# A four-layer graph network on one core: first weights loaded beside their zero blocks, layer 3's small weights ahead of the graph's second copy, pair 14's layer 3 by rows, both ends reordered

## The chip, the cores and the metric

The kernel runs on one core of a Trainium2 chip. The metric is the device time of one execution in microseconds (us), as the median of several runs.

## The reference, cut to what matters

The input `x` holds 32 batches of 512 nodes with 64 features; `adj` is one graph of 512 x 512 weights, mostly zeros. Four layers follow one another; each normalises its input, clips it at zero, and adds its result to it.

```
for f in (L0, L1, L2, L3):
    h = max(layernorm(x), 0);  x = x + f(h, adj)
L0: v = h, row 0 set to intervention_value
    3 times: v = relu([v, adj @ v] @ W1.T + b1) @ W2.T + b2
L1: 2 times: z = relu((adj @ z) @ weights[i])
L2: 8 heads: y = z @ Wh;  s = (y @ y.T) * adj, zeros -> -1e16
             head = softmax(s) @ y + bh
    cat = leaky(heads, 0.01);  once more such a layer, with W_out and b_out;  leaky 0.01
L3: adj's diagonal set to 1;  y = z @ weight
    e = leaky(y @ a[:64] (of the row) + y @ a[64:] (of the column), 0.2) * adj
    out = softmax(e) @ y + bias
```

## The kernel before, in words

Batches are handled in 16 pairs, numbered 0 to 15. All work is cut into small jobs with a pair and a name (`12.r4g`), and the order of the jobs is written out by hand, as three strings. `HEAD` lists the start (pairs 0 to 3), `ROUND` lists one steady round with a lag for each pair, and `TAIL` lists the end (from the middle of pair 12's heads on). The jobs issue their instructions in this order; each engine and each DMA queue then works through its own instructions in that order, so a job's place decides what waits behind it. `UNTIL` says up to which job a TensorE accumulator bank is held.

**Start.** `x` of pair 0 and the graph `A` are loaded on the SP queue, the weights `W1` and `W2` of layer 0 on the ACT queue. `W1n` and `W2n` hold each weight twice on the diagonal of a 128-wide tile, so GpSimd zeroes the two tiles first (L305) and the four loads follow (L310, L311). On SP follow the biases, `x` of pair 1, `NP`, `Wh`, then `A2` (a second copy of the graph, in another arrangement, L333), the small weights of layer 3 (`w3bd` L335, `a12` L337, six DMAs), `Wo_sb` (L338) and `A3` (a third copy, L340). The front of pair 0 runs batch by batch as two chains of 35 steps, `A0` to `A34` and `B0` to `B34` (layernorm, three steps of L0 with L648, L687 and L654 on TensorE, two of L1, layernorm, turning). The other pairs' fronts are `F0` to `F32`. `weights`, `joined`, `biases`, `bjoined`, `graph0` to `graph3` (L367: the graph turned), `masks`, `factor0` to `factor3` (L394, on `A2`), `loops0` to `loops3` (on `A3`), `grams` and `vectors` are one-time jobs; `vectors` (L425 to L436) makes layer 3's vectors out of `w3bd` and `a12`. `k`, `Y` make keys; the first attention scores are `0.s1a` and `0.s0a`.

**Attention of a unit** (letters `a` to `j`: pairs of heads; `f`: L2's output layer; `e`: L3). `s` are the scores in PSUM (L777 and the mask L780), `r` the product with the graph and the row maximum on VectorE (L786), `m` the negative on GpSimd (L799), `x` the exponentials with their sums on ScalarE (L806), `n` the division on GpSimd (L818), `t` 32 x 32 block transposes on VectorE (L824), `v` the weighing on TensorE with 32-row tiles (L833, L1061), from values that SP's DMAs have spread (`ZQ`, `hQ`, `lQ`). `w`, `y`, `o`, `c` apply `Wh`, bend, project with `W_out` and join. `f` and `h` make the operands of the output layer, `vAE`... `er` its sums, together with L3 of the pair before. `oA` to `oV` are L3's layernorm, turning and values; `oD`, `oF` and `de` send the column terms through DRAM into a broadcast tile `pd`, from which `s` of L3 is made on ScalarE (L1015).

**Last pairs.** Pair 15's output layer (`O0`, `O1`) and layer 3 (`L0`, `L1`) run by batch and *by rows*: 128 rows at a time, `s` from a `pd` that TensorE makes in PSUM (L1252, L1258), `r` with 128-row tiles of the graph (`aO`, `aL`, L1283), `m` on VectorE (L1141), `x` (L1145), `t` a full turn on TensorE (L1152), `e` its copy, half by ScalarE and half by VectorE (L1156, L1157), `v` the weighing with K = 128 (L1165), and the division on the way out (`z`, `q`, L1175, L1176). Layer 3 of pair 14 has no later pair to share its sums with, and runs alone by columns as the unit `e` does: `vAL` to `vDL` (L833, 128 columns), `lu` (L1026), `lt` (L491), `lr` (L1042).

Of the kernel before, what the change touches and what calls it, by code (L numbers as in the profile page):

```python
# [21 lines left out]
def gnn_stack_kernel(  # L22
# [50 lines left out]
        0.r2b 1.F7 0.ZQ02 0.m0a 0.r3b 0.r4a 0.ZQ12 0.x1a 0.x0a 0.nAa 0.r5a 0.m1b 0.s3a 0.t0a 1.F8 0.t1a 0.Y1 0.r6a
        0.r7a 0.s2b 0.ZQ01 0.r5b 0.r4b 1.F9 0.m2a 0.x1b 0.m3a 0.s0b 0.s3b 0.x3a 0.B33 1.F10 0.r0b 0.r1b 0.m2b 0.s3c
        0.r7b 0.ZQ00 0.m0b 0.x2a 0.r6b 0.B34 0.nBa 0.s0c 0.r7c 0.r6c 0.r1c 0.s1c 0.x0b 0.m3b 0.nAb 0.t2a 1.F11 0.r3c
        0.r0c 0.r2c 0.t3a 0.m1c 0.x3b 0.x2b 0.ZQ13 0.k2 0.m0c 0.x0c 0.loops3 1.F12 1.F13 0.nBb 0.t0b 0.t1b 0.s2c
        0.t2b 0.x1c 1.F14 0.ZQ03 0.s0d 0.t3b 0.m3c 0.nAc 0.r4c 0.Y2 0.r5c 0.r1d 0.vA0 0.r0d 0.m2c 0.s3d 0.s1d 0.r7d
        0.t0c 0.x2c 0.vB0 0.r3d 0.m0d 0.vC0 0.r2d 0.m1d 0.r6d 0.m3d 0.vD0 0.x0d 2.F1 0.x1d 0.x3c 0.nAd 0.t1c 0.s2d
        0.us0 0.s0g 0.w00 0.x3d 0.w10 0.nBc 0.r5d 0.r4d 0.m2d 0.y00 0.t1d 0.s1g 0.x2d 0.t0d 0.t2c 1.F15 0.r2g 0.nBd
        0.r3g 0.y10 0.t3c 1.F16 0.t2d 0.m1g 0.o0 0.t3d 1.F17 0.c0 1.F18 0.s3g 0.vA1 0.vB1 1.F19 0.r6g 0.x1g 0.r1g  # L80
        0.r0g 0.vC1 0.m0g 2.F2 0.vD1 0.x0g 0.loops2 0.ZQ10 0.s2g 1.F20 0.r7g 0.s0h 0.us1 0.r4g 1.F21 0.w11 0.r5g
        0.m2g 0.r1h 0.s2h 0.nAg 0.r0h 0.m3g 0.s3h 0.x2g 0.y11 0.k3 3.F0 0.m0h 0.r4h 0.x3g 0.r6h 1.F22 0.t0g 0.r5h
        0.Y3 0.m2h 0.s1h 0.nBg 0.r7h 0.t1g 0.x0h 1.F23 1.F24 1.F25 0.t2g 0.r3h 0.w01 0.r2h 0.s1i 0.m1h 0.y01 0.s0i
        0.x1h 0.x2h 0.t3g 0.r3i 0.ZQ11 0.o1 0.m3h 0.r2i 0.x3h 0.nAh 1.F26 0.r1i 0.r0i 0.c1 0.t0h 0.s3i 1.F27 0.nBh
        1.F28 0.t1h 0.t2h 0.t3h 0.m1i 0.s2i 1.F29 0.vA2 0.vB2 1.F30 0.r6i 0.r7i 0.m0i 0.r4i 0.D0 0.m3i 1.F31 0.vC2
        0.x1i 0.x3i 0.vD2 0.x0i 0.s2j 1.F32 0.r5i 3.F1 0.m2i 0.us2 0.nAi 1.zT 1.zE 0.s1j 1.ZQ01 0.x2i 0.r5j 0.r4j
        0.r2j 0.r3j 0.t1i 0.w12 0.y12 0.s3j 0.m1j 0.nBi 2.F3 0.x1j 2.F4 0.s0j 1.k0 0.r6j 1.Y0 0.m2j 0.w02 0.r0j
        0.hQ1 0.r1j 0.y02 0.r7j 0.t0i 1.s1a 1.r3a 2.F5 0.m0j 0.x0j 1.ZQ02 1.s3a 0.o2 2.F6 0.t3i 1.r6a 1.r2a 0.m3j
        1.s0a 3.F2 0.c2 0.nAj 0.t2i 1.r7a 0.x2j 1.k1 0.x3j 0.nBj 1.r1a 2.F7 2.F8 1.Y1 1.r0a 1.m1a 1.s0b 1.s2a 0.t1j
        0.t0j 1.m0a 1.m3a 0.t2j 0.t3j 0.vA3 1.x0a 1.r5a 1.r4a 1.s3b 1.r0b 1.r1b 1.s1b 0.vB3 1.x1a 1.m2a 1.x2a 1.nAa  # L90
        1.r6b 0.hQ0 0.vC3 1.r2b 1.r7b 1.r3b 1.m1b 0.vD3 1.t0a 1.m0b 1.t1a 1.x3a 1.x1b 1.s2b 1.nBa 1.x0b 1.s0c 1.r4b
        1.nAb 1.r5b 1.t2a 0.us3 0.w03 0.y03 1.s2c 1.r1c 0.w13 1.m2b 0.loops1 0.y13 1.r5c 1.m3b 1.r4c 2.F9 1.r0c
        1.t0b 1.m0c 1.s3c 1.x3b 2.F10 1.x2b 1.x0c 1.s1c 2.F11 1.r3c 0.o3 1.t1b 1.nBb 2.F12 1.r2c 2.F13 1.m2c 1.r6c
        1.ZQ03 1.r7c 1.m3c 1.t3a 1.t2b 1.m1c 1.t3b 1.ZQ00 0.c3 1.s0d 1.s1d 2.F14 1.x3c 1.vA0 1.x1c 1.x2c 1.vB0 1.r1d
        1.nBc 1.r3d 0.f1 1.r0d 1.s3d 0.D1 1.r2d 1.m1d 1.vC0 1.vD0 1.x1d 0.f0 1.nAc 1.t2c 1.m0d 1.r7d 0.hQ3 1.t1c
        1.s2d 1.r6d 1.x0d 0.s1f 1.nAd 1.us0 1.r4d 1.r5d 1.t0d 1.w10 0.s2f 1.t0c 1.y10 1.w00 1.y00 1.m2d 1.m3d 0.r3f
        0.r5f 1.t1d 1.x2d 2.F15 0.r4f 1.o0 1.x3d 1.t3c 1.nBd 0.r2f 2.F16 1.c0 1.ZQ13 0.s0f 1.t2d 2.F17 1.t3d 1.k2
        0.m1f 0.s3f 2.F18 0.m2f 0.r1f 1.Y2 4.F0 0.x1f 0.r0f 0.r7f 1.vA1 0.r6f 1.vB1 0.m0f 1.vC1 2.F19 4.F1 2.F20
        0.x0f 1.vD1 1.s1g 1.us1 1.r3g 0.m3f 1.r2g 1.k3 1.s0g 1.r0g 1.m1g 0.x2f 1.s3g 1.w11 2.F21 1.r1g 0.nAf 1.r6g
        1.r7g 1.Y3 1.s2g 1.s1h 1.w01 1.m3g 1.m0g 0.hQ2 1.r5g 1.r4g 0.x3f 0.nBf 1.r3h 1.y11 1.s2h 1.r2h 1.m2g 1.x0g  # L100
        1.x1g 1.x2g 1.y01 0.t0f 1.x3g 1.r4h 1.r5h 1.s0h 2.F22 0.t3f 2.F23 1.o1 1.ZQ12 0.t1f 1.nAg 1.r0h 2.F24 0.t2f
        1.m1h 2.F25 1.r1h 1.c1 1.m2h 1.x1h 1.m0h 1.s3h 1.t0g 0.vAE 1.r6h 1.nBg 1.r7h 1.x0h 1.t1g 1.m3h 0.vBE 1.x2h
        1.s1i 1.t2g 1.s0i 1.nAh 1.x3h 1.r2i 1.r0i 1.r1i 1.r3i 0.vCE 0.vDE 1.s2i 1.m1i 0.eu 1.nBh 2.F26 1.ZQ11 1.t0h
        1.t3g 1.t2h 2.F27 0.et 1.t3h 2.F28 1.t1h 0.er 2.F29 2.F30 1.s3i 1.x1i 1.r7i 1.ZQ10 1.m0i 1.vA2 1.r5i 1.r4i
        1.vB2 1.vC2 1.r6i 1.vD2 1.m2i 2.F31 1.s2j 1.D0 1.s1j 1.x2i 1.x0i 1.us2 2.F32 1.r5j 1.m3i 2.zT 3.F3 1.r2j
        1.s3j 1.nAi 2.zE 3.F4 1.r3j 1.r4j 1.t0i 1.w12 1.x3i 1.nBi 1.w02 1.r6j 1.m1j 1.f0 1.s0j 1.y12 2.k0 1.y02
        1.t1i 1.r0j 1.r1j 1.r7j 0.loops0 1.m2j 2.Y0 3.F5 1.t2i 1.m0j 2.s3a 1.x1j 1.m3j 2.s1a 2.r6a 2.r7a 1.hQ0 2.r3a
        1.x0j 2.r2a 1.t3i 1.o2 2.m1a 3.F6 1.x2j 1.x3j 1.hQ1 1.nAj 2.s0a 1.c2 2.r1a 1.nBj 2.r0a 1.t0j 2.k1 1.t1j
        2.m3a 1.t2j 2.s2a 2.Y1 1.t3j 2.r4a 2.m0a 3.F7 2.r5a 2.ZQ02 2.m2a 3.F8 2.x3a 2.x0a 0.oA 2.s0b 1.vA3 2.r1b
        2.r0b 2.x1a 2.nAa 2.x2a 0.oB 2.m0b 2.nBa 1.vB3 2.ZQ03 1.vC3 1.vD3 1.us3 2.s1b 3.F9 2.t0a 1.w03 1.y03 2.t1a  # L110
        2.r2b 2.r3b 3.F10 2.s3b
# [27 lines left out]
        12.r4g 11.nBf 12.r6g 11.t0f 11.t1f 11.t2f 12.r5g 13.F23 12.x1g 12.c1 12.m3g 11.t3f 13.F24 14.F2 12.s0h  # L139
        12.r0h 12.m2g 13.F25 12.r1h 10.lQ2 12.m0h 12.x2g 12.s1h 12.nAg 11.vAE 12.r3h 12.r2h 12.t0g 12.x3g 12.m1h  # L140
        12.x0h 11.vBE 12.nBg 12.t1g 11.vCE 12.x1h 11.vDE 15.aO1 12.t2g 12.s3h 12.nAh 12.t3g 12.r7h 12.s2h 12.r6h
        12.r4h 12.r5h 11.eu 12.t0h 12.k3 12.t1h 11.et 12.m3h 12.Y3 12.m2h 11.er 12.s0i 12.r1i 12.x2h 12.s1i 12.x3h
        12.nBh 13.F26 12.r3i 12.r0i 12.r2i 12.s3i 13.F27 12.m0i 12.t2h 13.F28 12.t3h 13.F29 12.s3j 12.vA2 12.m1i
        13.F30 12.vB2 12.r7j 13.F31 12.vC2 12.vD2 12.r7i 12.x0i 12.x1i 12.r6j 12.s2i 13.F32 12.r6i 12.us2 13.zT
        12.r4i 12.f0 12.r5i 12.m3i 13.zE 12.s0j 12.s2j 12.m2i 14.F3 12.r1j 12.x3i 12.nAi 12.r4j 12.r5j 12.x2i 12.s1j
        14.F4 12.t0i 15.aL3 13.k0 13.Y0 13.ZQ00 12.m2j 12.r0j 12.w12 13.ZQ02 12.nBi 13.s3a 15.aO2 12.w02 12.t1i
        12.r3j 12.y12 12.m3j 13.r6a 12.m0j 14.F5 13.s2a 12.x2j 12.r2j 12.y02 13.r7a 12.m1j 12.x0j 13.m3a 13.s0a
        12.D0 12.t3i 13.r5a 13.r4a 12.o2 13.r0a 12.hQ0 13.s1a 13.r1a 12.x1j 13.s3b 12.x3j 12.c2 12.nAj 14.F6 12.t2i
        13.r2a 13.m2a 13.r3a 13.x3a 13.x2a 12.nBj 13.k1 13.r6b 13.r7b 12.t1j 13.m1a 13.m3b 12.t0j 13.m0a 13.nBa
# [154 lines left out]
    for z0 in (W1n, W2n):  # L304
        nc.gpsimd.memset(z0, 0.0)  # L305
# [3 lines left out]
    for r in R:  # L309
        nc.scalar.dma_start(out=W1n[r, :, r], in_=W1.rearrange("o (k d) -> o k d", k=2))  # L310
        nc.scalar.dma_start(out=W2n[r, r], in_=W2)  # L311
# [20 lines left out]
    for r in R:  # L332
        nc.sync.dma_start(out=A2[r], in_=adj.rearrange("(s q) m -> q s m", q=D))  # L333
# [1173 lines left out]
```

## Time and profile before

| | |
|---|---|
| runs shown | 2047.02, 2047.13, 2048.74 us; median 2047.13 |
| profiled execution, its own time | 2046.44 us |
| its span | 2044.7 us (1.7 us lie around it) |
| TensorE busy | 1998.0 us, 98% |
| VectorE, ScalarE, GpSimd busy | 1818.6, 1497.2, 1289.9 us |
| granted TensorE clock, mean | 0.992 |

Rows of windows give, for a stretch of the span: its length, then the busy time and instruction count of each engine, the granted TensorE clock, the busy share of the DMA engines, and GB/s. Rows of the timeline give start, length, engine, line, operation, tile written and read, count, and in brackets the idle time of the engine before it and what ended it. The chain of waits is followed back from the last instruction. Several matmuls are recorded twice (one of 512 columns in four-byte numbers counts as two).

### The profile page before, as it was taken

To read this page: it belongs to the slowest core of one execution; us is meant where nothing else is said; L and a number is where in the kernel's file an instruction comes from. 1 tells how busy PE (TensorE), PEld (TensorE's weight loads), DVE (VectorE), ACT (ScalarE), POOL (GpSimd) and SP (SyncE) were. 2 spreads that over 40 slices of the span, in tenths; PEclk is the share of its full clock that TensorE was granted. 3 is DMA by queue.
4 is the path that set the end of the run, shared out by engine and by line. 5 is a ranking of instruction groups with operands and counts; after the bars stand their busy time and mean duration, and the time that the engine had idled before them with its cause. 6 is when DMAs were issued, how large, how long until landed. Compare 5 with 4: busy or idle time off the path is not lost.

```text
span 2044.7 us, 90579 instructions
## 1 busy us (share of the span) xinstructions
PE 1998.0 (98%) x38701; PEld 1196.2 (59%) x38701; DVE 1818.6 (89%) x4247; ACT 1497.2 (73%) x3866; POOL 1289.9 (63%) x2193
## 2 busy tenths in 40 slices
PE   6999999999999999999999999999999999999997
PEld 4555565665656556565665655566565565655555
DVE  4888889999898999989999998999989899899967
ACT  1567668777787777878777787877778677787856
POOL 2476665766667575776658666675766567566541
PEclk9999999999999999999999999999999999999998
DMA  6101111102121110212111121111112111022101
GB/s 140 28 2 31 26 31 36 38 20 44 25 43 29 34 38 17 45 28 41 34 29 34 26 44 29 37 37 25 39 26 42 41 34 32 16 46 44 38 15 37
DMA packets 247224, 71.61 MB, mean 35 GB/s; under 512 B 230052, under 2 KB 239396, under 8 KB 246820
## 3 DMA queue, kind: packets, MB, share of 16 engines
q1 hardware_dynamic: 246368, 65.72, 15.5%
q8 instruction: 303, 4.96, 1.0%
q14 instruction: 101, 0.83, 0.1%
q10 hardware_dynamic: 452, 0.10, 0.0%
HBM read 14.49 MB, written 4.26 MB: 9 GB/s over the span
## 4 chain that ended last, share of the span: by engine, by line
PE 91%; DVE 4%; ACT 2%; POOL 1%; DMA 1%; issue 1%; SPq 0%; ACTq 0%; POOLq 0%; DVEq 0%
PE s L777 24%; PE mm L833 23%; PE s L780 6%; PE mm L894 5%; PE mm L536 5%; PE mm L874 5%; PE mm L1061 5%; PE mm L513 5%; PE mm L1294 3%; PE mm L539 2%; DVE sm L786 2%; PE mm L561 2%; DVE sm L824 2%; PE mm L501 1%; PE mm L530 1%
## 5 line engine op out<-in xcount | busy, mean ns | idle before, releaser
L806 ACT ACTIVATE sm<-sm,nmx 128x512 f32<-128x512 f32 x1264 | 898.3, 717 | 162.6 <-POOL nmx L799 161.0
L818 POOL TENSOR_SCALAR sm<-sm,rs 128x512 f32<-128x512 f32 x1264 | 852.3, 693 | 223.4 <-DVE rs L816 193.3
L786 DVE CUSTOM_DVE_ANT_0 sm<-s,A 128x512 f32<-128x512 f32 x1264 | 804.4, 679 | 43.6 <-PE s L780 39.9
L824 DVE STREAM_TRANSPOSE sm<-sm 128x1024 f32<-128x1024 f32 x632 | 765.3, 1229 | 52.5 <-POOL sm L818 49.6
L777 PE MATMUL s<-ZZ,Y 64*64 64x512 f32 x3840 | 510.8, 596 | 1.1 <-ACT Y L1305 0.9
L833 PE MATMUL mm<-sm,vq 32*64 32x256 f32 (+1 forms) x16640 | 484.0, 377 | 5.7 <-DVE sm L824 5.3
L833 PEld LDWEIGHTS mm<-sm,vq 32*64 32x64 f32 x16640 | 382.1, 132 | 120.6 <-issue 49.3
L799 POOL TENSOR_SCALAR nmx<-mx 128x2 f32<-128x2 f32 x632 | 128.6, 214 | 325.6 <-DVE mx L786 293.4
L806 ACT ACTIVATION_READ_ACCUMULATOR sm<-sm,nmx 128x1 f32 x1264 | 244.1, 193 | 0.0
L780 PE MATMUL s<-NEGM,I2b 64*64 64x512 bf16 x2288 | 237.1, 377 | 0.0
L777 PEld LDWEIGHTS s<-ZZ,Y 64*64 64x64 f32 x3840 | 131.3, 133 | 144.7 <-issue 64.8
L886 ACT ACTIVATE y<-mm,cols 128x512 f32<-128x512 f32 x256 | 161.3, 687 | 30.8 <-PE mm L874 30.8
L780 PEld LDWEIGHTS <-I2b 64*64 64x64 bf16 x2288 | 78.5, 107 | 153.3 <-issue 152.7
L456 POOL TENSOR_TENSOR r<-ve,mhalf 128x8 f32<-128x8 f32 (+1 forms) x68 | 108.3, 1593 | 89.1 <-DVE ve L454 84.8
L874 PE MATMUL mm<-us,Wh 64*64 64x512 f32 x1024 | 132.9, 590 | 0.9 <-ACT us L868 0.9
L868 ACT COPY us<-mm 128x256 f32<-128x256 f32 x256 | 76.0, 381 | 73.2 <-PE mm L833 73.0
L894 PE MATMUL mm<-y,Wo_sb 128*64 128x256 f32 x1024 | 124.1, 384 | 2.5 <-ACT Y L1305 2.5
L1061 PE MATMUL mm<-sm,vq 32*64 32x256 f32 x3712 | 111.0, 376 | 1.4 <-POOL nmx L799 0.2
L513 PE MATMUL mm<-AT,z 128*128 128x512 f32 x240 | 111.0, 605 | 0.1
L536 PE MATMUL mm<-AT,v 128*64 128x256 f32 x960 | 110.2, 382 | 0.0
L1061 PEld LDWEIGHTS mm<-sm,vq 32*64 32x64 f32 x3712 | 99.9, 132 | 16.2 <-PE s L780 7.9
L786 DVE DVE_READ_ACCUMULATOR2_ANT mx<- 128x1 f32 x1280 | 106.3, 83 | 0.0
(203 smaller groups left out, 1961.7 us busy)
## 6 DMA issues: line engine op xcount, KB each, us to landing
vq<-z SPq DMA_DIRECT2D x512, 32.0 KB
HH<-cat SPq DMA_DIRECT2D x128, 64.0 KB
vq<-catT SPq DMA_DIRECT2D x240, 32.0 KB
vq<-h3n SPq DMA_DIRECT2D x240, 32.0 KB
A<-in_adj_dram SPq DMA_DIRECT2D x5, 1024.0 KB
xt<-in_x_dram SPq DMA_DIRECT2D x32, 128.0 KB
ZZ<-ZZ SPq DMA_DIRECT2D x30, 128.0 KB
pd<-dst SPq DMA_DIRECT2D x30, 128.0 KB
```

Of the source, the lines that this page charges most:

```text
L513: nc.tensor.matmul(pe, lhsT=v[:, m].rearrange("p j d -> p (j d)"), rhs=AT[:, m, :], start=(m == 0), stop=(m == NT - 1),)
L536: nc.tensor.matmul(ph[out_, :], lhsT=v[:, m, j, :], rhs=AT[:, m, h], start=False, stop=stop)
L777: nc.tensor.matmul(pss[half][R[ab], :], lhsT=lhsT, rhs=rhs, start=True, stop=False)
L780: nc.tensor.matmul(pss[half][R[ab], :], lhsT=I2b[R[half], :], rhs=NEGM[R[half], k, :], start=False, stop=True)
L786: nc.vector.tensor_tensor_reduce(self.sm[:, s, :], self.pss.pop(s), self.graph(s), 1.0, -FMAX, ALU.mult, ALU.max, self.small("mx", slice(s ...
L806: nc.scalar.activation(self.sm[:, s, :], self.sm[:, s, :], AF.Exp, bias=self.small("nmx", slice(s, s + 1)), accum_out=self.small("ssum", s ...
L818: nc.gpsimd.tensor_scalar(self.sm[:, s, :], self.sm[:, s, :], self.small("rs", slice(s, s + 1)), 1.0, ALU.mult, ALU.mult)
L824: nc.vector.transpose(out=two, in_=two)
L833: nc.tensor.matmul(self.u[i][R[c], 0 : weights.shape[1] * 32], lhsT=values[32 * i : 32 * i + 32, jb, :], rhs=weights[32 * i : 32 * i + 32, ...
L874: nc.tensor.matmul(self.py[ab][c][r, :], lhsT=Wh2[R[c], self.head(c, ab), r], rhs=self.us[R[c], 2 * ab : 2 * ab + 2].rearrange("p i (s e) ...
L894: nc.tensor.matmul(self.pa[R[half], 0 : N // 2], lhsT=Wo_sb[:, self.head(k, ab), :], rhs=self.y[self.head(k, ab)][:, half * N // 2 : (half ...
L1061: nc.tensor.matmul(self.u[i][r, 0 : N // 2], lhsT=values[q, jb, :], rhs=unit.sm[q, :, 32 * jb : 32 * jb + 32], start=(jb == 0), stop=(jb = ...
```

## The change: what it does

1. The zero blocks of `W1n` and `W2n` are filled beside the weights, not under them; the four loads no longer follow the fill.
2. On SP the six DMAs of `w3bd` and `a12` are issued ahead of the two of `A2`.
3. Layer 3 of pair 14 runs by rows, as new units `M0` and `M1` of the class `HalfLast`. Its `oD`, `oF`, `de`, `e` jobs, `lQ` and `vAL` to `lr` are gone.
4. `HEAD` and `TAIL` are written anew; `ROUND` is the same. `vectors` moves from its place between `0.B4` and `0.B5` to the late part of `HEAD` (pair 1's heads).

```diff
-    for z0 in (W1n, W2n):
-        nc.gpsimd.memset(z0, 0.0)
+    for r, other in zip(R, R[::-1]):
+        nc.scalar.dma_start(out=W1n[r, :, r], in_=W1.rearrange("o (k d) -> o k d", k=2))
+        nc.scalar.dma_start(out=W2n[r, r], in_=W2)
+        nc.gpsimd.memset(W1n[r, :, other], 0.0)
+        nc.gpsimd.memset(W2n[r, other], 0.0)
     make_identity(nc, ident)
...
-    for r in R:
-        nc.scalar.dma_start(out=W1n[r, :, r], in_=W1.rearrange("o (k d) -> o k d", k=2))
-        nc.scalar.dma_start(out=W2n[r, r], in_=W2)
...
-    for r in R:
-        nc.sync.dma_start(out=A2[r], in_=adj.rearrange("(s q) m -> q s m", q=D))
     for j, r in enumerate(R):
         nc.sync.dma_start(out=w3bd[r, r], in_=w3)
         for k in range(2):
             nc.sync.dma_start(out=a12[r, 2 * k + j : 2 * k + j + 1], in_=a3[k * D : (k + 1) * D, :])
+    for r in R:
+        nc.sync.dma_start(out=A2[r], in_=adj.rearrange("(s q) m -> q s m", q=D))
...
+            if self.p == NPAIR - 2:
+                for j, pn in enumerate(self.pns):
+                    s["src", j] = st.tile([P, NT], F32, tag="src", bufs=4, name="src")
+                    nc.vector.tensor_copy(s["src", j], pn[:, :, D])
+                    nc.scalar.copy(h3n[:, :, j, :], pn[:, :, :D])
+                    s["h3n", j] = h3n[:, :, j, :]
+                return
...
     class HalfLast(Half):
         def targets(self):
             self.pd = score_ps()
+            own = R[self.j] if self.p < NPAIR - 1 else R[0]
             for r in R:
                 nc.tensor.matmul(
-                    self.pd[r, :], lhsT=w3d[R[0], R[0]], rhs=state[self.p]["zT3", self.j], start=True, stop=True
+                    self.pd[r, :], lhsT=w3d[own, own], rhs=state[self.p]["zT3", self.j], start=True, stop=True
                 )
...
+                first = HalfLast(p - 1, j, "M", "rowsL", "h3n")
+                job(p, f"dM{j}", first.targets)
+                job(p, f"b3M{j}", first.biased)
...
-        unit_jobs(p, "e", last)
-        job(p, "de", last.targets)
+        if p < NPAIR - 2:
+            unit_jobs(p, "e", last)
+            job(p, "de", last.targets)
...
-        if p == NPAIR - 2:
-            sum_jobs(p, "L", last)
-            for name, fn in (("lu", last.evict), ("lt", last.rows), ("lr", last.residual)):
-                job(p, name, fn)
```

The new start up to the first scores, and the stretch of the new end around pair 15's last join:

```
0.A0 0.B0 0.weights 0.A1 0.joined 0.A2 0.A3 0.A4 0.biases 0.B1 0.A5 0.A6 0.graph2 0.graph1 0.graph3 1.F0
0.graph0 0.bjoined 0.B2 0.A7 0.B3 0.A8 0.A9 0.B4 0.A10 0.B5 1.F1 0.B6 0.A11 0.masks 0.B7 0.A12 1.F2 0.A13
0.B8 0.A14 0.A15 0.factor0 0.A16 0.B9 0.A17 0.B10 0.B11 0.A18 0.A19 0.B12 0.B13 0.A20 0.B14 0.B15 0.factor3
0.A21 0.A22 0.B16 0.factor1 0.A23 0.B17 0.B18 0.A24 0.A25 0.A26 0.A27 0.B19 0.A28 0.grams 0.B20 0.loops2
0.A29 0.A30 0.A31 0.loops1 0.B21 0.A32 0.B22 0.B23 0.A33 0.A34 0.B24 2.F0 0.B25 0.k0 0.B26 0.Y0 0.factor2
0.ZQ00 0.B27 2.F1 0.ZQ03 0.s1a 0.s0a
...
14.oC 15.w03 15.w13 15.r3O0 15.y03 15.y13 15.t0O0 15.x2O0 15.m3O0 15.e0O0 14.oT 14.oE 15.o3 14.oN 15.t1O0
15.dM0 15.x3O0 15.c3 15.t2O0 14.oV 15.e1O0 15.t3O0 15.s2M0 15.e2O0 15.e3O0 15.v0O0 15.v2O0 15.r2M0
```

The first scores stood in the old `HEAD` behind `0.B30` and `1.F5`. In the old `TAIL` pair 13's layer 3 began `13.de 15.y00 13.s3e 15.t3d 13.r3e 13.s7e 13.r7e`; in the new it begins `13.de 14.m1f 15.w00 15.w10 15.y00 15.nBd 14.r6f 15.y10 15.t1d 15.k3 15.t2d 15.Y3 13.s0e 15.t3d 13.s3e 13.r0e`, and its eight `r` stand ahead of `14.s0f`.

## The prediction

> **What bounds the kernel now.** The page first: TensorE is busy for nearly the whole span, so the time is its work plus the places where it stands still or runs slowly.
>
> ```profile
> PE 1998.0 (98%) x38701; PEld 1196.2 (59%) x38701; DVE 1818.6 (89%) x4247; ACT 1497.2 (73%) x3866; POOL 1289.9 (63%) x2193
> ```
>
> TensorE idles for 2044.7 - 1998.0 = 46.7 us. The waits of TensorE between 100 and 1850 us sum to 2.7 us, so nearly all of it lies at the two ends. The windows of the start:
>
> ```profile
> 0.00:8.30 8.30, 0.00 (x0) 0.01 (x1) 4.28 (x13) 1.77 (x3) 3.81 (x16) 1.00 0.60 170
> 8.30:23.50 15.20, 12.62 (x96) 8.95 (x96) 6.60 (x17) 2.31 (x7) 3.69 (x5) 1.00 0.80 168
> 23.50:28.60 5.10, 0.06 (x3) 0.05 (x1) 0.25 (x1) 0.63 (x2) 0.00 (x0) 0.97 1.03 148
> 28.60:36.00 7.40, 6.81 (x57) 3.83 (x57) 2.59 (x10) 0.66 (x3) 3.14 (x3) 0.56 0.98 218
> ...
> 50.00:66.30 16.30, 12.70 (x258) 8.18 (x255) 11.49 (x30) 4.17 (x12) 5.28 (x4) 1.00 0.05 10
> ```
>
> TensorE stands for 5.0 us before 28.6, and works at a clock of 0.56 in the 7.4 us behind it. Its waits name the causes, and the chain of waits shows that the second one sets the end:
>
> ```profile
> PE mm L357 <- DMA early<-in_L_gnn_b_dram: 8.3, 1, 8.3
> PE mm L427 <- DMA early<-in_L_gnn_weight_dram: 5.0, 1, 5.0
> PE mm L367 <- DVE b1s L387: 2.2, 1, 2.2
> ```
> ```profile
> 17.42 10.92 DMA early<-in_L_gnn_weight_dram
> 28.34 0.25 issue
> 28.58 0.46 PE mm L427
> ```
>
> L427 is `vectors`, standing in TensorE's order ahead of pair 0's front, and its weight is queued behind the 2 MB of `A2`. From 66.3 to 100 us TensorE is busy for 33.35 of 33.7 us. The windows of the end:
>
> ```profile
> 1905.00:1911.00 6.00, 3.26 (x19) 0.71 (x14) 6.00 (x16) 4.95 (x9) 1.05 (x4) 0.84 0.22 46
> 1911.00:1916.30 5.30, 4.92 (x32) 2.29 (x40) 5.02 (x15) 5.30 (x15) 1.14 (x4) 0.54 0.26 53
> ...
> 1987.50:2002.00 14.50, 13.05 (x104) 8.82 (x97) 8.33 (x38) 7.47 (x24) 0.00 (x0) 1.00 0.28 66
> 2002.00:2011.00 9.00, 6.12 (x42) 4.71 (x43) 8.48 (x31) 8.94 (x24) 2.17 (x4) 0.83 0.34 73
> 2011.00:2020.00 9.00, 4.07 (x20) 2.27 (x16) 8.52 (x18) 5.80 (x15) 6.25 (x10) 0.50 0.00 1
> 2020.00:2026.70 6.70, 6.24 (x249) 6.00 (x250) 4.11 (x16) 2.66 (x7) 1.73 (x2) 0.62 0.02 5
> ```
>
> Pair 15's last join (`c3`) ends at 1987.5. In the 57.2 us behind it TensorE works 43.6 us (the four rows from 1987.5, 10.81 to 2038, 3.31 to the end). Between 2011 and 2026.7 the column form of pair 14's layer 3 holds it up, as the timeline shows:
>
> ```profile
> 2016.05 2.69 POOL L818 TENSOR_SCALAR sm<-sm,rs 128x512 f32<-128x512 f32 x4 [0.75 <-DVE src L1244]
> ...
> 2020.07 6.21 PE L833 MATMUL mm<-sm,vq 32*64 32x128 f32 x248 [1.97 <-DVE sm L824]
> ...
> 2026.67 0.63 PE L1222 MATMUL mm<-ident,z 128*64 128x128 f32 x4 [0.39 <-ACT yT L1026]
> ```
>
> Division on GpSimd, block turns on VectorE and 256 small matmuls follow one another; pair 15's last turn (L1222), whose operand is ready at 2023.4, stands behind them.
>
> **The first weights.** Their loads start on the ACT queue at 1.06 behind the fill; SP's first load starts at 0.72. At most 0.3 us goes; 1 MB of `A` is queued in between and the landing at 8.2 follows that, so I take 0.3, between 0 and 1.5 (`z` of the first batch is ready at 7.5, 1.7 us before its turn at 9.2). The smaller fills cost nothing: GpSimd then idles for 2.9 us before 5.26.
>
> **Layer 3's small weights ahead of `A2`.** SP spends 0.90 + 1.76 + 0.59 + 1.23 = 4.5 us on the six, so `A2` issues at 17.7, not 13.2. The DMA engines are full until about 28, so it lands between 28 and 30. Behind it on SP are `Wo_sb`, `A3` and pair 2's `x`, needed much later. `factor0` on VectorE is first to read `A2`; the old order reached it at 37.2, the new one some 8 us earlier, about when `A2` lands. If the landing is later, pair 0's front waits behind it for up to 2 us; taken at nothing, since the windows leave VectorE idle for over half of 28.6 to 36.
>
> **`vectors` moved.** The wait goes (5.0), and so does 28.34 to 30.76, 2.4 us, of which 0.46 + 0.56 + 0.63 = 1.65 us of matmuls stay, now where TensorE is full: 0.8 net. With the gap goes the slow clock: in the chain the next 64 x 64, 64 x 256 and graph matmuls took 0.64 + 0.85 + 3.34 where the same later took 0.46 + 0.43 + 1.88: 2.1 us. [...]
>
> **The start reordered.** `F0`, which kept VectorE waiting for pair 1's `x`, now stands behind three of the graph's turns: 2.2 us of L367's wait go. What is late next is batch A's own chain. The first scores now stand ahead of `B28`, `F3` and `F5`, so 0.46 + 0.65 + 0.77 us of filler and the 1.65 of `vectors` are missing from the stretch that already idles 3.6 of 16.3 us. I give back 2.4 us, nearer to the 2.6 idle in 8.3 to 23.5; the ends are 0 and 7.4, double that idle. Start: 0.3 + 5.0 + 0.8 + 2.1 + 2.2 - 2.4 = **8.0**, between 3.0 and 10.4.
>
> **The end up to `c3`.** Between 1898 and 1916.3 TensorE idles 0.88 + 2.74 + 0.38 = 4.0 us, and the 4.92 us at clock 0.54 hold 4.92 x 0.46 = 2.3 too much. VectorE waited there for `pd` of pair 13 (landing at 1905.05) with other maxima behind it. The new order puts 0.62 + 3 x 1.16 = 4.1 us of VectorE work between the issue and the first maximum, but then eight maxima (5.0 us) ahead of `14.s0f`, against 1.9 + 0.9 of projection and keys on TensorE. I take **2.5** of the 6.3, with ends +6.3 and, if a like stall arises in another pair, -4.
>
> **Pair 14 by rows.** TensorE loses L833 7.1, L491 0.6, L979 0.3. It gains eight turns at 0.55 (L1152 x8 took 1.09), eight weighings at 0.92 (32 records took 3.68) and two `dM` at 1.03 (L1252 at full clock): 4.4 + 7.4 + 2.1. That is **5.9 us more** on the bounding engine, and not hidden by itself. VectorE: L824 4.9, L816, L963, L984, L1042 out (6.5); L1157, L1141, L1175, L1176 in (3.3 + 1.2 + 1.2 + 2.3 + 0.3): +1.8. ScalarE: +3.1 copies, -1.1. GpSimd loses 5.7. On SP 23 DMAs go (four `src`, one `dst`, two `pd`, sixteen `lQ`), which stood ahead of later graph rows. The gain is in waits: the first score can follow `oV` (1989.3) instead of `pd` (2002.6), and nothing needs division or block turns before weighing. Behind `c3`: 43.6 + 5.9, less 2.2 for the clock (L1252 1.97 against 1.03, L1232 1.97 against 1.10, L1222 1.02 against 0.63), less 2.1 of turns and `dM0` now ahead of `c3`, where TensorE is full, is 45.2; VectorE has 39.3 + 1.8 = 41.1. Idle was 13.6, of which 3.4 (last row and store) stay; I add 3.6 for hand-overs between the three interleaved chains, nearest to the 1.45 and 2.88 idle of the first two rows. 45.2 + 7.0 + 2.1 = 54.3 against 57.2: **2.9** gained; with idle 4.0 it is 5.9, with 13.6 it is 3.7 lost. A new wait: `r2M0` on VectorE stands behind `oV` and ScalarE's `s2M0`, and `O0`'s divisions and `O1`'s maxima queue behind it; should it come late, the hand-over falls into the 3.6.
>
> [...]
>
> **Sum.** 8.0 + 2.5 + 2.9 = 13.4. The profiled execution took 2046.4 (span 2044.7, 1.7 around it), so 2033.0; the median of the runs is 0.7 above it, so **2033.7**.
>
> **The rivals.** *A, the row form pays for nothing:* its 5.9 us stay and the idle time with them, because maxima of three units now share VectorE, already 8.5 of 9 busy from 2002 on, and `dM0` and `dM1` hold two of the four score buffers. 8.0 + 2.5 - 3.7 = 6.8: 2040.3. *B, another wait takes the place of `vectors`:* batch A's chain of copies and layernorms binds. 3.0 + 2.5 + 2.9 = 8.4: 2038.7. For it: the 3.6 us idle at 50 to 66.3 are such waits. *C, both ends at their best:* 10.4 + 6.3 + 5.9 = 22.6: 2024.5. *D, slower:* in the new `TAIL` the run of eight maxima with four block turns, 8 x 0.67 + 4 x 1.2 = 10.2 us on VectorE, starves TensorE in two more of the pairs 11 to 13: 20.4 - 8.0 - 2.9 = 9.5 slower, 2056.6. It decides once new idle time before `c3` exceeds 10.9 + 4.1. For it: VectorE is busy for 51 of 55.7 us from 1916 to 1972. Against: TensorE's waits in the old order show one such place. *E, gains and the 5.9 cancel:* 2047.
>
> **How the numbers follow.** Forecast 0.52 (own range 2028 to 2038), A 0.13, B 0.13, C 0.10, D 0.07, E 0.05. The range 2022 to 2043 leaves out D, E and the far side of C, some 0.15. About 0.2% (4.1 us) can be told from no change: faster than 2043.0 are the forecast, B, C and most of A, 0.86; E and the rest of A 0.07; slower 0.07.
>
> **What would show it.** Right: no TensorE wait on the weight's DMA near 28 us, a clock of 0.9 or more from 28 to 36, first scores near 58 (66.3 before); idle under 3 us around pair 13's layer 3; L833 gone behind `c3`, TensorE near 50 us busy in the last 54. Wrong: first scores after 63, a wait for `A2` in VectorE, a new wait of TensorE for L786 between 1600 and 1987, or over 10 us idle behind `c3`.

## The result and the profile after

The changed kernel takes 2039.3 us (median of 5 runs, 2037.58 to 2040.0); the kernel before took 2048.35 us beside it. The ratio is 0.9955, 95% interval 0.9944 to 0.9966: 9.05 us faster, where 13.4 were forecast. The profiled execution took 2039.3 us, span 2037.5.

Busy time by engine, from the page of the changed kernel:

```profile
PE 2000.8 (98%) x38541; PEld 1209.2 (59%) x38541; DVE 1815.7 (89%) x4269; ACT 1501.8 (74%) x3870; POOL 1289.7 (63%) x2185
```

TensorE works 2.8 us more than before and idles 2037.5 - 2000.8 = 36.7 us, 10 less. The windows of the start (length, busy time of each engine, granted clock, DMA share, GB/s):

```profile
8.30:23.50 15.20, 13.09 (x137) 9.80 (x139) 8.90 (x25) 3.31 (x10) 4.63 (x6) 1.00 0.68 134
23.50:28.60 5.10, 5.10 (x58) 2.74 (x56) 2.34 (x5) 1.58 (x3) 3.88 (x3) 1.00 1.08 213
28.60:36.00 7.40, 5.28 (x85) 2.93 (x83) 4.05 (x11) 0.95 (x2) 0.55 (x1) 1.00 1.13 212
36.00:54.00 18.00, 15.33 (x252) 10.16 (x245) 11.62 (x29) 4.72 (x11) 6.42 (x12) 1.00 0.38 68
54.00:66.30 12.30, 12.30 (x200) 8.17 (x202) 10.81 (x35) 8.33 (x23) 5.63 (x11) 1.00 0.16 32
```

The 5 us hole ahead of 28.6 and the clock of 0.56 behind it are gone, and the first scores stand at 54.0 in place of 66.3. Between 8.3 and 66.3 TensorE now idles 6.9 us; it was 12.8. The longest waits of TensorE up to 100 us (total, times, longest one), and the chain of waits with the graph's second copy in it:

```profile
PE mm L360 <- DMA early<-in_L_gnn_W_dram: 8.3, 1, 8.3
PE mm L690 <- DVE v L686: 1.4, 1, 1.4
```
```profile
17.88 13.15 DMA A<-in_adj_dram
31.08 0.04 issue
31.12 1.23 DVE A L397
32.35 0.21 DVE v L686
32.60 0.65 PE mm L690 x4
```

Two readings: the first weights still hold TensorE to 8.3 us, and `factor0` (L397) now waits for `A2`, which costs TensorE 1.4 us (L690). The end behind `c3` of pair 15 as one row of the windows, first before and then after:

```profile
1987.50:2044.70 57.20, 43.59 (x526) 34.30 (x518) 39.34 (x139) 35.26 (x95) 10.15 (x16) 0.83 0.17 39
```
```profile
1985.20:2037.50 52.30, 45.71 (x366) 36.44 (x355) 37.21 (x160) 34.96 (x94) 4.13 (x5) 0.98 0.07 16
```

This stretch is 4.9 us shorter: 2.1 us more busy time on TensorE, 13.6 us of idle time down to 6.6. But `c3` itself comes only 2.3 us sooner than before, although the start gave 9. The longest waits of TensorE in `TAIL` ahead of `c3`, before (1640 to 1987) and after (1640 to 1985), and the two places of the new kernel in the timeline:

```profile
PE s L777 <- DVE mx L786: 3.1, 2, 2.3
```
```profile
PE s L780 <- DVE mx L789: 4.2, 3, 3.2
PE mm L1281 <- ACT yT L1061: 2.2, 1, 2.2
```
```profile
1703.75 1.58 PE L1281 MATMUL mm<-ZZ,G 64*64 64x256 f32 x13 [2.17 <-ACT yT L1061]
...
1909.48 2.58 PE L780 MATMUL s<-HH 64*64 64x512 f32 x8 [3.17 <-DVE mx L789]
```

The stall at pair 13's layer 3 is still there (3.17 us in one piece; 3.1 in two before), and a new one of 2.17 us stands at pair 13's `k3`.

How early each kernel reaches the same points shows where time is won and lost. The points are the starts of VectorE's add `c1` or `c3` (L908 before, L911 after), read from each trace; a negative number is earlier than before, in us. Start alone, end alone and rows in old places are experiments told of below.

| point | before, at | start alone (e1) | both (after) | end alone (e2) | rows in old places (e5b) |
|---|---|---|---|---|---|
| pair 11 `c3` | 1527.0 | -8.4 | -9.0 | +1.2 | +0.8 |
| pair 13 `c1` | 1700.0 | -8.3 | -7.6 | +2.5 | +0.9 |
| pair 13 `c3` | 1774.7 | -8.3 | -4.2 | +4.3 | +0.9 |
| pair 14 `c3` | 1886.5 | -8.2 | -1.0 | +8.2 | +1.2 |
| pair 15 `c1` | 1935.5 | -8.1 | -3.8 | +6.2 | +2.1 |
| pair 15 `c3` | 1987.1 | -8.1 | -2.3 | +7.7 | +2.1 |
| from there to the end | 57.6 | 57.2 | 52.7 | 52.7 | 60.0 |

`TAIL` begins behind the first row. In it the changed kernel loses 6.7 us up to `c3` (9.0 to 2.3), and behind `c3` it wins 4.9.

### The profile page after: what moved, and what is told of

Same layout as the page of the kernel before. It is cut to its first block, busy times and chain, and to the rows that moved or that the text cites. A ratio compares the mean times of both kernels' runs of the same rounds, so it can differ in the third digit from the quotient of the medians.

```text
span 2037.5 us, 90271 instructions
## 1 busy us (share of the span) xinstructions
PE 2000.8 (98%) x38541; PEld 1209.2 (59%) x38541; DVE 1815.7 (89%) x4269; ACT 1501.8 (74%) x3870; POOL 1289.7 (63%) x2185
## 4 chain that ended last, share of the span: by engine, by line
PE 93%; DVE 4%; DMA 1%; ACT 1%; issue 0%; SPq 0%; ACTq 0%; DVEq 0%
PE s L780 24%; PE mm L836 23%; PE s L783 6%; PE mm L1044 5%; PE mm L897 5%; PE mm L516 5%; PE mm L539 5%; PE mm L877 5%; PE mm L1281 3%; PE mm L542 3%; DVE sm L789 2%; PE mm L564 2%; DVE sm L827 1%; PE mm L504 1%; PE mm L1148 1%; PE mm L533 1%
## 5 line engine op out<-in xcount | busy, mean ns | idle before, releaser
L780 PE MATMUL s<-ZZ,Y 64*64 64x512 f32 x3840 | 518.0, 597 | 2.1 <-ACT Y L1292 1.1
L836 PE MATMUL mm<-sm,vq 32*64 32x256 f32 x16384 | 475.9, 376 | 0.7 <-DVE rs L819 0.4
L783 PE MATMUL s<-NEGM,I2b 64*64 64x512 bf16 x2288 | 244.4, 376 | 0.0
L780 PEld LDWEIGHTS s<-ZZ,Y 64*64 64x64 f32 x3840 | 135.4, 133 | 148.1 <-issue 61.8
L1044 PE MATMUL mm<-sm,vq 32*64 32x256 f32 x3712 | 111.5, 376 | 1.8 <-issue 0.2
```

Source lines behind the costliest of these rows:

```text
L780: nc.tensor.matmul(pss[half][R[ab], :], lhsT=lhsT, rhs=rhs, start=True, stop=False)
L783: nc.tensor.matmul(pss[half][R[ab], :], lhsT=I2b[R[half], :], rhs=NEGM[R[half], k, :], start=False, stop=True)
L836: nc.tensor.matmul(self.u[i][R[c], 0 : weights.shape[1] * 32], lhsT=values[32 * i : 32 * i + 32, jb, :], rhs=weights[32 * i : 32 * i + 32, ...
L1044: nc.tensor.matmul(self.u[i][r, 0 : N // 2], lhsT=values[q, jb, :], rhs=unit.sm[q, :, 32 * jb : 32 * jb + 32], start=(jb == 0), stop=(jb = ...
```

## The experiments

Kernels of one set shared the runs of the kernel before: medians 2048.51 (e1 to e4), 2047.53 (e5 to e8) and 2047.87 us (f1 to f3 and e5b). All edits of order move names in the strings.

**e1_start and e2_end: the change cut in two.** e1 is before with the new loads and the new `HEAD`; e2 is before with pair 14 by rows and the new `TAIL`.

```diff
 e1_start, against before
+ items 1 and 2 (loads)     + new HEAD      (old TAIL, pair 14 by columns)
 e2_end, against before
+ item 3 (rows)             + new TAIL      (old loads, old HEAD)
```

> The kernel before with the new start alone (first weights beside their zero blocks, small weights ahead of A2, the new HEAD); TAIL and pair 14's layer 3 by columns as before. Theory 1 (the start and the end are separate accounts: a lead of 9 us from pair 3 on is the start's, and what is lost of it later is lost by the new TAIL): 9.2 us faster, about 2039.1. Theory 2 (the end is paced by VectorE and does not move when the start does, so most of the lead is eaten there whatever the order): 2 to 4 us faster, about 2045.

> The kernel before with pair 14's layer 3 by rows and the new TAIL alone; loads and HEAD as before. Theory 1: 4.9 us gained behind pair 15's last join, 6.7 lost ahead of it: 1.8 us slower, about 2050. Theory 2: the 4.9 are kept and little is lost: 4 to 5 us faster, about 2044. The prediction's own terms (2.5 + 2.9) say 5.4 faster.

e1: 2038.91 us, ratio 0.9958 (0.9945 to 0.997). e2: 2049.62 us, ratio 1.0012 (1.0003 to 1.0021). The start is the whole gain; the end alone is slower by 0.6 to 4.3 us. The start alone and the whole change can't be told apart (0.9958 and 0.9955). The table shows how: e1 keeps its 8 us to the last `c3`, the whole change spends 6.7 of its 9.0 on the way there and gets 4.5 us (57.2 against 52.7) back behind it. The two profiled spans differ by 1.3 us, in e1's favour.

**e3_w3 and e4_vec: what the start's gain is made of.** The hole had two possible remedies, and the change applies both.

```diff
 e3_w3, against before
-    (A2's two loads)
     for j, r in enumerate(R): (w3bd and a12, six loads)
+    (A2's two loads)
 e4_vec, against before
-        0.A8 0.B4 0.vectors 0.B5
+        0.A8 0.B4 0.B5
-        0.t3f 2.F23 1.o1
+        0.t3f 2.F23 0.vectors 1.o1
```

> The kernel before with the six small DMAs ahead of A2 alone; all orders as before. If the queue is the cause of TensorE's 5.0 us wait at 23.5, w3bd lands near 19 and the wait and the slow clock go: 5.0 + 2.1 = 7.1 faster, about 2041. If another wait of pair 0's front takes its place (A2 is then 2 us later, batch A's own chain): 3 faster, about 2045.

> The kernel before with the job vectors moved to the late part of HEAD alone (behind 2.F23); DMA order as before. Theory 1: 5.0 + 2.1 + 0.8 = 7.9 faster, about 2040.5. If the wait is only replaced: 3 faster, about 2045. Close to the run with the small DMAs moved alone, if both remove one and the same wait.

e3: 2040.53 us, ratio 0.9966 (0.9953 to 0.9978). e4: 2042.44 us, ratio 0.9973 (0.9963 to 0.9983). The windows of e3, then of e4:

```profile
23.50:28.60 5.10, 4.56 (x49) 2.68 (x47) 2.25 (x9) 0.90 (x3) 0.53 (x1) 1.00 1.07 218
28.60:36.00 7.40, 7.22 (x100) 3.86 (x98) 3.17 (x9) 2.05 (x4) 3.40 (x3) 1.00 1.13 205
```
```profile
23.50:28.60 5.10, 4.18 (x66) 2.23 (x66) 1.28 (x5) 1.37 (x4) 1.65 (x1) 1.00 1.12 173
28.60:36.00 7.40, 7.40 (x90) 4.14 (x92) 4.23 (x10) 1.58 (x3) 2.28 (x2) 1.00 0.85 188
```

Each alone fills most of the hole (TensorE busy for 4.56 and 4.18 of 5.10 us) and brings the clock back to 1.00. Together with the order they give 9.6 us (e1), not the 14 that 8.0 and 6.1 make: the same wait is removed twice. e3 shows that the weight was late only by the queue's order, a small load behind 2 MB; e4 shows that TensorE had other work ready behind `vectors`.

**e8_A2: the price of `A2`'s later landing.** The changed kernel with item 2 undone.

```diff
+    (A2's two loads)
     for j, r in enumerate(R): (w3bd and a12, six loads)
-    (A2's two loads)
```

> The changed kernel with A2's two loads back in front of layer 3's six small ones; the new order of the start stays, in which factor0 stands early and vectors late. After: 2039.3. Theory 1 (A2's later landing costs the start 1.4 us through factor0, which the prediction took at nothing): 1.4 faster, 2037.9, first scores 1 to 1.5 us sooner than 54.0. Theory 2 (batch A's own chain sets the first scores): within 0.5 us of 2039.3, first scores at 54.

First scores at 52.2, no wait of L690, and pair 11's `c3` 1.5 us sooner than in the changed kernel. So the 1.4 us were paid in the start. The time is 2039.62 us, ratio 0.996 (0.9948 to 0.9972). That interval is 4.9 us wide, so 1.4 us can't be seen in it either way. In the profiled executions nothing is left of them: the spans are 2037.5 and 2037.6. The lead is still 1.6 us at pair 14's `c1`, 1.0 at its `c3`, and 0 at pair 15's `c1`; between the last two lies the stall at 1906 us. The windows there, of the changed kernel and of e8:

```profile
1900.00:1908.00 8.00, 6.30 (x69) 3.07 (x60) 8.00 (x16) 7.90 (x16) 3.11 (x6) 1.00 0.27 65
1908.00:1916.00 8.00, 6.52 (x112) 4.17 (x120) 6.25 (x22) 7.55 (x20) 1.63 (x6) 0.79 0.24 49
```
```profile
1900.00:1908.00 8.00, 4.94 (x56) 2.41 (x50) 8.00 (x20) 7.92 (x14) 2.88 (x5) 0.97 0.30 69
1908.00:1916.00 8.00, 7.90 (x112) 4.31 (x120) 4.92 (x18) 7.55 (x22) 2.13 (x7) 0.60 0.24 49
```

The wait is 3.2 us in both, but the slow clock takes 8 x 0.21 = 1.7 us in one and 8 x (0.03 + 0.40) = 3.4 in the other (0.1 and 0.3 of which fall into the wait itself). So in these two executions the clock took back what was left of the lead. That they stand for all runs is not shown.

**e5_rows and e5b_look: the row form without the new order.** Old start, old order, with pair 14's layer 3 by rows in the places of its column jobs.

```diff
-        ... 14.oD ... 14.oF ... 14.de ... 14.s4e ... 14.vAL ... 14.lu 14.lt ... 14.lr
+        ... 15.dM0 (for de) ... 15.dM1 15.s0M1 ... 15.b3M0 15.b3M1 15.v0M0 15.v1M0 ... 15.q2M1 15.q3M1
```

> The kernel before with pair 14's layer 3 by rows and nothing else: loads, start and the order of the end stay as they were, and the row form's steps stand where the column form's stood (dM0 in the place of de, dM1 ahead of the place of s4e, the score, maximum, turn and weighing steps of each tile where the column's were; aL0 and aL2 ahead of 14.oV). Before: 2048.5. Theory 1 (the row form pays by its shorter chain, and the small loss of the whole end lies in its new order ahead of c3): the last 57 us shorten by 3 to 5, so 2043.5 to 2045.5. Theory 2 (its 5.9 us of TensorE work are not covered, as rival A had it): 0 to 4 slower, 2048.5 to 2052.5. Rows decide too: idle time of TensorE behind c3 13.6 before, near 7 by theory 1.

> The same kernel as e5_rows (old start, old order of the end, pair 14's layer 3 by rows), for one readable profile; its time is 2050.2 against 2047.5 before. Theory 1: the stretch behind c3 shortens as in the changed kernel (57.2 to about 52.3) and the loss lies ahead of c3, where dM0's scores and pair 15's units stand in places made for the column form. Theory 2: the row form itself costs time behind c3, which then stays at 57 or grows, with TensorE's idle time near 13.6 or more.

e5_rows: 2050.18 us, ratio 1.0012 (1.0003 to 1.0021), slower by 0.6 to 4.3. e5b_look is the same kernel, a single run of 2050.94 us; the profile is taken from it. The stretch behind `c3` there, and a part of it:

```profile
1989.60:2049.20 59.60, 49.79 (x368) 40.21 (x358) 38.21 (x161) 36.43 (x99) 4.79 (x6) 0.94 0.10 23
```
```profile
2012.00:2025.00 13.00, 11.17 (x65) 9.20 (x62) 9.16 (x36) 10.83 (x30) 0.00 (x0) 0.74 0.01 2
```

The stretch grows, as theory 2 has it: TensorE's busy time goes from 43.6 to 49.8 us, and the shorter chain takes only 3.8 us of idle time away (13.6 to 9.8), so it is 2.4 longer. The longest waits are hand-overs from VectorE and ScalarE between the three interleaved chains (1.8, 1.0 and 1.0 us). The form by itself does not pay.

The short end of the changed kernel comes only with its order. It is not short because much work was done sooner: nearly the same matmuls stand behind `c3` in both, 366 records in the changed kernel and 368 in e5b. In the changed kernel they take 45.7 us of TensorE, in e5b 49.8. Four records of turns, 0.7 us, run ahead of `c3` in the changed kernel, and e5b has a slow clock from 2012 to 2025, 13 x 0.26 = 3.4 us, which the changed kernel has not. And TensorE idles 6.6 us in the changed kernel, 9.8 in e5b. So the new order brings fewer waits and, in the profiled execution of the changed kernel, the full clock while TensorE works (granted 1.00 from 1985.2 to 2035.5; the last matmul ends at 2034.1). It pays for that ahead of the last `c3`, which comes 7.7 us late in e2 and 2.1 late in e5b. In the time the two cancel: form and order together (e2) and the form alone (e5) have the same ratio, 1.0012.

**e6_eu and f1_k3: the new stall at `k3`.** I first read the 2.17 us as ScalarE's queue: `12.eu`, which empties the sums' accumulator banks, stands behind pair 13's exponentials.

```diff
 e6_eu, against after
-        12.vDE 13.x1h 13.D0 13.nAg 13.x3h 13.ZQ12 13.nAh 12.eu 13.t2g 13.t0g 13.nBh 13.t0h 13.k3
+        12.vDE 12.eu 13.t2g 13.x1h 13.D0 13.nAg 13.x3h 13.ZQ12 13.nAh 13.t0g 13.nBh 13.t0h 13.k3
 f1_k3, against after
-        12.vAE ... 12.vDE ... 12.eu ... 13.k3 12.et 13.t1g 13.Y3 13.t1h 13.t3g 13.s0i 13.s1i 12.er
+        13.k3 13.Y3 12.vAE ... 12.vDE ... 13.s0i 12.eu ... 13.s1i 12.et 13.t1g 13.t1h 13.t3g 12.er
```

> The changed kernel with pair 12's eu (ScalarE's eviction of the layer-3 sums) moved to directly behind 12.vDE, ahead of pair 13's weighted sums x1h and x3h. After: 2039.3. Theory 1 (TensorE's stall of 2.2 us at 1701.6 and the slow clock behind it are paid in the time): 2.2 + 1.5 us faster, 2035.6. Theory 2 (the time is taken by the next wait of the same stretch, for VectorE's maxima): within 1 us of 2039.3, with the idle time at another line of pair 13.

e6: 2044.45 us, ratio 0.9985 (0.9977 to 0.9994): 4.8 us slower than e8, which ran beside it and is as fast as the changed kernel. The timeline (lines are 7 higher here):

```profile
1702.42 1.55 ACT L1065 ACTIVATE yT<-mm,cols 64x256 f32<-64x256 f32 x4 [3.08 <-PE mm L1051]
...
1704.50 1.91 PE L1288 MATMUL mm<-ZZ,G 64*64 64x256 f32 x13 [2.17 <-ACT yT L1068]
...
1707.11 0.18 DVE L826 RECIPROCAL rs<-ssum 128x4 f32<-128x4 f32 x1 [8.03 <-ACT sm L816]
```

`eu` can't start before the sums end (L1051), so ScalarE stood for 3.08 us ahead of it with the exponentials behind it, and VectorE waited 8.03 us for them. TensorE's wait stayed at 2.17. My reading was wrong. The next one was that `k3` waits for a bank of PSUM (one of the accumulator banks of `UNTIL`) that the sums hold until `eu` empties it.

> The changed kernel with pair 13's k3 and Y3 moved ahead of 12.vAE, and s0i and s1i moved to directly behind the sums, ahead of 12.et. The theory behind e6_eu fell: eu did not wait in ScalarE's queue, it waited for the sums themselves (256 matmuls, 7.46 us, end 1701.6), and k3 waited for the banks that the sums hold until eu has emptied them. Theory 1 (banks): without k3 behind the sums the stall of 2.2 us at 1701.6 goes and with it 1.7 us of slow clock: 3.5 to 4 faster than after, 2035.5. Theory 2 (the stretch is bound by something else, ScalarE's or VectorE's own chain): within 1 us of 2039.3, the idle time at another line of pair 13.

f1: 2040.0 us, ratio 0.9962 (0.9948 to 0.9976), as the changed kernel. The wait at `k3` is gone, as the reading by banks says, and it is back from the other side: the sums now wait for the bank that `Y3` has to empty.

```profile
1694.63 0.65 PE L1051 MATMUL mm<-sm,vq 32*64 32x256 f32 x4
1696.79 9.32 PE L1051 MATMUL mm<-sm,vq 32*64 32x256 f32 x252 [1.52 <-ACT Y L1299]
```

That is 0.65 us less of waiting, but here the slow clock falls on the sums (granted 0.83 from 1692 to 1702), 9.32 us against 7.46: pair 13's `c3` comes 0.6 later than in the changed kernel.

**e7_run and f2_sums: the stall at pair 13's layer 3.** Eight scores, eight maxima and eight rows of exponentials follow one another there. e7 puts other scores ahead of them; f2 puts pair 15's sums beside them.

```diff
 e7_run, against after
-        15.Y3 13.s0e 15.t3d 13.s3e ... 13.lQ2 14.s0f 14.hQ1 13.m3e 14.s2f 15.c0 ... 15.vA1
+        15.Y3 14.s0f 15.t3d 15.o0 14.s2f ... 15.k2 15.Y2 15.c0 ... 15.vA1 13.s0e 13.s3e ...
 f2_sums, against after
-        13.s0e 15.t3d ... 14.s0f 14.hQ1 13.m3e 14.s2f ... 15.vA1 ... 15.vD1 ... 15.s0g 15.us1
+        13.s0e 15.t3d ... 15.c0 15.k2 ... 15.vA1 ... 15.vB1 ... 15.vD1 13.m3e 13.x1e 14.s0f ... 14.s2f 15.us1 ...
```

> The changed kernel with the scores and maxima of pair 13's layer 3 put behind pair 14's s0f, s2f, m0f, m2f and pair 15's k2, Y2, c0 and vA1, so that the eight maxima no longer stand ahead of 14.s0f. After: 2039.3. Theory 1 (the predicted gain of the end up to c3 failed because the stall at pair 13's layer 3 stayed, 3.2 us idle and 1.7 us of slow clock): 4 to 5 us faster, 2034.3 to 2035.3, and no wait of L780 for L789 near 1906. Theory 2 (the stall is VectorE's own work, 51 of 55 us busy there, so the wait only moves): within 1 us of 2039.3, with a wait of the same size at a later line of pairs 13 to 15.

e7: 2044.43 us, ratio 0.999 (0.998 to 1.0): again 4.8 us slower than e8. The timeline:

```profile
1908.43 4.98 ACT L1033 ACTIVATE s<-pd,src 128x512 f32<-128x512 f32 x8
...
1923.88 3.69 PE L884 MATMUL mm<-us,Wh 64*64 64x512 f32 x16 [5.82 <-ACT us L878]
```

The old wait is gone, and pair 15's sums, ready early, ran at 1908 us. But then ScalarE made the eight scores (4.98 us) and behind them 14 exponentials of 0.71 us, and `us1`, which empties the sums' banks, stood behind them all: 5.82 us. The wait moved and grew.

> The changed kernel with pair 15's sums vA1 to vD1 (7.6 us of TensorE, ready near 1907 in the run e7_run) put ahead of 14.s0f, so that TensorE has work while pair 13's layer 3 runs its eight scores and eight maxima, and us1 put ahead of the last layer-3 exponentials, so that it does not queue behind all of them as it did in e7_run (5.8 us). Theory 1 (the eight units are a lump that costs what TensorE has nothing beside): the 3.2 us wait near 1906 and 1.7 us of slow clock go: 4 to 5 faster than after, 2034.5 to 2035.5. Theory 2 (the lump only moves, as in e7_run): 2039 to 2044, with a wait of 2 us or more at another line between 1900 and 1930.

f2: 2046.3 us, ratio 0.9995 (0.9986 to 1.0004). With the sums ahead of `14.s0f`, the maxima of pair 14's output layer begin 7 us later. VectorE idles for 7.21 us, and TensorE then waits 4.61 for it:

```profile
1919.73 0.69 DVE L796 CUSTOM_DVE_ANT_0 sm<-s,A 128x512 f32<-128x512 f32 x1 [7.21 <-PE s L790]
...
1929.94 2.87 PE L787 MATMUL s<-ZZ,Y 64*64 64x512 f32 x6 [4.61 <-DVE mx L796]
```
```profile
1930.00:1940.00 10.00, 10.00 (x44) 3.74 (x48) 7.83 (x18) 4.93 (x12) 4.16 (x9) 0.50 0.12 26
```

Behind the wait TensorE works for 10 us at a clock of 0.50, which takes another 5.0 us. Pair 15's `c1` comes 10.9 us later than in the changed kernel (9.8 of them since pair 14's `c3`). The profiled execution took 2050.16 us, near the top of the runs (2043.87 to 2050.27), so most runs lose less than it shows. The wait moved, as theory 2 has it, and the time lies above the 2044 that it allowed.

**f3_both: all three mends.** f1, f2 and e8 in one kernel.

> f1_k3 and f2_sums together, with A2's two loads in front of the six small ones as in e8_A2. If the three are independent and each pays: 3.9 + 4.5 + 1.4 below after, 2029.5. If the lump moves or the slow clock comes back at another stall: 2034 to 2038. No gain over after would mean that TensorE's waits are not what the end pays for.

2047.45 us, ratio 0.9996 (0.9987 to 1.0005). Pair 14's `c3` is 2.3 us earlier than in the changed kernel: e8 alone made it 1.0 earlier, f1 alone 1.0 later, but the slow clock that f1 had at the sums is absent here (granted 1.00 from 1690 to 1710). Pair 15's `c1` is 7.3 later, so what f2 moved outweighs the rest. None of these kernels beats the start alone or the whole change.

## Why the prediction was right and where it was wrong

The sign, the size of the start and the stretch behind `c3` were right; 9.05 us were gained where 13.4 were forecast, because one term had the wrong sign. (Of the 5.6 us between 2033.7 and 2039.3, 1.2 are the kernel before, which took 2047.13 when the forecast was made and 2048.35 beside the changed kernel.) In the profiled executions the terms came out so: the start 9.0 where the sum had 8.0; the end up to `c3` 6.7 lost where the sum had 2.5 won less 2.1 of work moved there, 0.4 won; behind `c3` 4.9 won where it had 5.0.

**The start, 8.0: 9.0 measured** as the lead at pair 11's `c3` (8.4 in e1, whose median time is 9.6 us shorter). The wait for the weight's DMA went as worked out. Idle time from 8.3 to 66.3 fell by 12.8 - 6.9 = 5.9 us. The mis-sized term is the slow clock, 2.1 in the sum: the 6.81 us at clock 0.56 held 6.81 x 0.44 = 3.0. First weights, 0.3: nothing, since the loads start at 0.73 in place of 1.06 but the first matmul still starts at 8.3; the landing does not follow the fill. That it follows what else is queued is not shown. `factor0`'s wait for `A2`, taken at nothing with up to 2 and named among the signs of being wrong: 1.4, as `A2` landed at 31.08 and not by 30. The argument that VectorE is idle for half of that stretch was beside the point: in the chain above `L686` on VectorE and `L690` on TensorE stand behind the waiting `L397`, however idle the engine is. First scores at 54.0, not 58.

**The end up to `c3`, a gain of 2.5: the step that failed.** The stretch lost 6.7. The prediction took 2.5 of a 6.3 us stall as won, because `pd` would have more time to land. The traces show the stall standing there after the change, 3.17 us and 1.7 of slow clock. VectorE is busy throughout it (8.00 of 8.00 us in the row from 1900 to 1908, and on to its end at 1909.5), so it is not a late `pd` that holds VectorE up there, but the maxima and turns that stand in its order; e7 and f2 show the wait move when they are moved. So this term was about nothing. What was lost came on top, and from pair 11's `c3` to pair 15's it looks so, before and after:

```profile
1526.99:1987.09 460.10, 452.16 (x8992) 266.62 (x8988) 413.75 (x958) 349.96 (x902) 288.52 (x503) 0.99 0.16 34
```
```profile
1518.04:1984.83 466.79, 456.61 (x8996) 271.66 (x8992) 413.72 (x959) 353.03 (x908) 290.22 (x505) 0.99 0.17 35
```

TensorE idles 2.2 us more (7.9 to 10.2). That is as much as the new wait at `k3`, a stall of the kind that the prediction left at the end of its range ("if a like stall arises in another pair"). And TensorE is busy for 4.5 us more, with only four more records: they are the four turns that run ahead of `c3`, 0.7 us. The 2.1 of the sum was too much, for `dM0` starts at 1985.9, behind `c3`. The slow clock took about as much in both (6.8 us at 0.50 each: from 1909.0 to 1915.9 before, from 1704.5 to 1707.9 and from 1909.3 to 1912.7 after). In the other 3.5 us or so the same matmuls, each as long as before (598 and 601 ns for 944 records of scores), run less side by side: as a group these scores keep TensorE busy for 134.3 us in place of 128.2. Why the new order has that effect is not settled, and e6 to f3 show only that mending a single place does not give the loss back.

**Pair 14 by rows, 2.9 behind `c3`:** the numbers of the sum came true almost exactly, 45.7 us of TensorE's work against 45.2 and 6.6 idle against 7.0 (the 50 us named among the signs contradicted the sum). That is partly luck, since 1.4 of the 2.1 us of work to be moved stayed behind `c3`. And the reason did not hold. The sum put the gain to the form; e5 shows that the form alone is slower (2050.18 us against 2047.53), that its work stays, as rival A said, and that the shorter end needs the new order. (The new order with the old form was not run.) The order's price ahead of `c3` stood in the sum only as 2.1 us of moved work.

**Rivals.** B's time, 2038.7, is nearest to the measured 2039.3, by luck: the chain of batch A left 9.0, not 3.0, so B is out. A's time, 2040.3, is 1.0 off; its work stays, but not the idle time (13.6 before, 9.8 in e5b, 6.6 in the changed kernel). D was right that the new `TAIL` costs time ahead of `c3`, but not by starving TensorE in two more pairs: the idle time rose by 2.2, not by 15.

**The clock.** From 2020 to 2031 of the changed kernel, where 24 of TensorE's 102 records are the row form's turns, the granted clock was 1.00; so it was in the kernel before from 2026.7 to 2038 (36 turns in 88 records). Both stretches hold other matmuls beside the turns, so what clock turns alone would be granted is not shown.

## What to carry to other kernels

Two remedies for one wait do not add: ask of each whether it alone removes the wait, and count it once. A stretch that got shorter is not a gain until the point where it begins has been compared too; here 4.9 us behind `c3` came with 6.7 lost ahead of it, and a table of the same points in several kernels shows that at a glance. Fewer microseconds of busy time are not less work: the same matmuls took 45.7 us in one order and 49.8 in another. In an order in which several engines run without slack, mending the largest visible wait moved it to the next shared buffer or queue (e6, f1, e7, f2). Cutting the lump of eight units smaller was not tried here.

## What the runs showed of the hardware

In these profiles the slow clock behind a wait did not go by the wait's length. Behind waits of 3.2 us at the same place it took 1.7 us in the changed kernel, 3.4 in e8, and nothing in f1, whose windows are the first two below; the third is f1 at its wait of 1.52 us:

```profile
1904.00:1912.00 8.00, 4.84 (x52) 2.27 (x48) 8.00 (x18) 7.46 (x14) 2.56 (x7) 1.00 0.28 58
1912.00:1920.00 8.00, 8.00 (x259) 6.07 (x259) 6.18 (x16) 8.00 (x23) 5.34 (x12) 1.00 0.24 47
1692.00:1702.00 10.00, 8.48 (x186) 5.56 (x186) 6.47 (x17) 9.28 (x26) 7.47 (x14) 0.83 0.01 2
```

So behind a wait of half the length it took 10 x 0.17 = 1.7 us. In f2 (the row from 1930 to 1940) the clock was 0.50 for 10 us behind a wait of 4.61, although TensorE was busy all the while. What sets how long the slow clock lasts these runs do not show.
